# Planning the first sequence's start on one NeuronCore: two halves side by side, earlier constants

## The chip, the core and the metric

The kernel runs on one core of a Trainium2 chip. The core has five engines that run their own instruction streams in order and wait for one another by semaphores: TensorE (PE, matmuls), VectorE (DVE, elementwise work and scans), ScalarE (ACT, activations), GpSimd (POOL) and SyncE (SP), which here only starts DMA transfers. ScalarE and GpSimd start some transfers too. The metric is the device time of one execution in microseconds, and lower is better. The profiler's span runs from the first instruction to the last; a little lies around it.

## The reference

Eight sequences of 256 tokens with 512 features pass two layers. Each layer has a recurrence over time ("wkv") fed by a layer norm and a context, and a feed-forward block fed by another layer norm. In layer 0 the feed-forward block is a gated one whose down weights carry a Walsh-Hadamard transform; in layer 1 it is a mixture of 8 experts, of which each token uses two.

```python
x = x + tanh(g_xattn[0]) * wkv(w0, u0, layernorm(x), ctx)        # scan over 256 steps
x = x + tanh(g_ffn[0])   * ffn_hadamard(layernorm(x), W1, W2, W3) # hidden 2048
x = x + tanh(g_xattn[1]) * wkv(td1, tf1, layernorm(x), ctx)
x = x + tanh(g_ffn[1])   * experts(layernorm(x), gate_w, w1, w2, w3)  # top 2 of 8
```

One step of `wkv`, per channel:

```python
no = maximum(o, u + kt); A = exp(o - no); E = exp(u + kt - no)
y = (A * p + E * vt) / (A * q + E)
no2 = maximum(w + o, kt); A2 = exp(w + o - no2); E2 = exp(kt - no2)
p, q, o = A2 * p + E2 * vt, A2 * q + E2, no2
```

All is in float32. The Hadamard transform of 2048 values is folded into W2 on the chip, in two passes of 128x128 matrices: the first works on W2 in one layout of its rows and writes the result to a scratch tensor in DRAM, the second loads it back in the other layout.

## The kernel before

**Tiling.** Activations lie transposed: 512 features as 4 chunks of 128 partitions, tokens along the free side. Sequence 0 is worked in two blocks of 128 tokens (b = 0, 1; `NB` = 2), the later sequences whole. The recurrence of a block falls into two halves of two feature chunks each (hf = 0, 1); block 1 continues from the `carry` of block 0.

**Loads.** `load_first` (L218) brings x and the context of sequence 0, block by block, on SP's queue. Sixteen loads of W2 follow (L275), then the constants by `load_const` (L261), which are issued from ScalarE's queue, then W1 and W3 in sixteen pieces of 512 KB (`fill_w13`, L237, L241), then x of sequence 1 (`load_x`, L208). The stores of the first Hadamard pass into `turned` (L578), the loads from it (`fill_w2`, L249) and the clearing of the expert queues (`clear_queues`, L320) are on SP too.

**Steps.** `layernorm` (L374) is a chain through four engines: two adds on VectorE (L379, L381), a mean by a matmul (L385), a subtraction (L387), a Square on ScalarE (L391), two adds (L395, L397), a variance by a matmul (L404), an addition (L409), a power on GpSimd (L411), a transpose on TensorE (L416) and a product on VectorE (L418). `decayed_max` (L472) is one half of layer 0's recurrence: maximum scans (L490), a difference (L495), Relus and exponentials on ScalarE (L502 to L516), two clamps (L511), a product (L514), two scans (L519, L521) and a sum (L529); `attend` (L448) ends it with a reciprocal on VectorE (L460), two steps on GpSimd (L454, L456) and two more on VectorE (L464, L466). `transform` (L564) is one matmul of a Hadamard pass and its copy back by ScalarE (L570). `unit` (L739) is one hidden unit of the feed-forward block: eight matmuls (L746) and the gating on ScalarE and VectorE (L753, L755, L757).

**Order.** All these are generators that yield the engine and the estimated length of the next step. In a stretch under `tc.manual_schedule` the order in which the program writes the instructions is the order on the engines it names. For the first sequence's beginning (from L1303) that order is written out by hand: the norm of block 0, its halves step by step, then groups of first-pass Hadamard products between steps of the halves, with block 1's norm in between, then the norm of block 0 for the feed-forward block mixed with the beginnings of block 1's halves. `set_up` (L340) stands in the middle of it with the preparation of later constants. From L1330 on, a planner takes over. It keeps a `clock` for each engine and a list of `Line`s (L140), each one a generator with the time at which its next step can start. `product` (L192) writes the next matmuls of the feed-forward block and moves TensorE's clock on; `fill` (L176) then writes steps of the other engines that would start before that clock, the earliest first. `finish` (L184) writes a line to its end. The gating of a unit is a line put first in the list. For sequence 0 (`first_ffn_hidden`, L774) all sixteen units are computed for block 0, then `rest`, what is left of block 1's halves and its norm, is finished, and the sixteen units of block 1 follow, between which the second Hadamard pass is written. `ahead` is the recurrence and norm of the next sequence, `centre_gate` (L363) subtracts the mean of the expert gate's columns.

The hand-written order at its core:

```python
for n, hf in ((4, 0), (2, 0), (2, 1), (2, 0), (2, 1)):
    run(fw, n)            # n first-pass Hadamard products
    run(half[0][hf], 1)   # one stage of a half of block 0
    run(norm[1], 1)       # one stage of block 1's norm
```

Of the kernel before, what the change touches and what calls it, by code (L numbers as in the profile page):

```python
# [8 lines left out]
FP = mybir.dt.float32  # L9
# [41 lines left out]
def flamingo_kernel(  # L51
# [31 lines left out]
    def v4(name, shape=(P, DC, T)):  # L83
        return work.tile(list(shape), FP, tag="v4", name=name, bufs=35)
# [29 lines left out]

    clock = dict.fromkeys("PAVGD", 0.0)
    banks = [0.0, 0.0]
    lines = []
    LATER = 1e9  # L120
    SLACK = 0.8

    def pe(width, n=1, bank=False):
        return "P", n * max(0.28, 0.00169 * width), bank

    def dve(width, slope=1.0):
        return "V", 0.09 + 0.00105 * slope * width, False
# [9 lines left out]
    def dma(length):  # L137
        return "D", length, False

    class Line:  # L140
        def __init__(self, *gens, first=False):
            self.gen = chain(*gens)
            self.at = clock["P"]
            self.bank = None
            self.first = first
            lines.insert(sum(line.first for line in lines) if first else len(lines), self)
            self.go_on()


        def go_on(self):  # L150
            self.op = next((op for op in self.gen if op is not None), None)
            if self.op is None:
                lines.remove(self)

        def starts(self):
            return max(self.waits(), clock[self.op[0]])
# [4 lines left out]

        def write(self):
            engine, length, bank = self.op
            end = self.starts() + length
# [8 lines left out]
            self.go_on()  # L173


    def fill():  # L176
# [4 lines left out]
            lines[min(ready)[1]].write()  # L181


    def finish(line):  # L184
        while line in lines:
            if line.starts() >= LATER:
                next(other for other in lines if other.bank is not None).write()
            else:
                line.write()


    def product(length, write):  # L192
# [22 lines left out]
        return t  # L215


    def load_first():  # L218
        x[0], t = v4("x0"), v4("c0_0")
        for b in range(NB):  # L220
            bs = slice(b * P, (b + 1) * P)
            nc.sync.dma_start(out=x[0][:, :, bs], in_=x_in[:, :, bs])
            nc.sync.dma_start(out=t[:, :, bs], in_=ctx_in[:, :, bs])
        return t

# [32 lines left out]
    def w2_of(w, k):  # L258
        return w[k // 2][:, k % 2, :]
# [3 lines left out]
        nc.scalar.dma_start(out=t, in_=src)  # L263
        return t

    first_ctx = load_first()

    w2h = [new_w2(n) for n in "ab"]
    turned = dram.tile([H0, D], FP, name="turned")
# [3 lines left out]

    for i in range(16):
        nc.sync.dma_start(out=w2_of(w2h[i // KC], i % KC), in_=by_kj(W2T, i))  # L275
    wcol = [load_const(w0, [P, DC], "w0c"), load_const(td1, [P, DC], "w1c")]
    ucol = [load_const(u0, [P, DC], "u0c"), load_const(tf1, [P, DC], "u1c")]
    tgx = load_const(g_xattn.partition_broadcast(P), [P, 2], "tgx")
    tgf = load_const(g_ffn.partition_broadcast(P), [P, 2], "tgf")
    hadm = load_const(had, [P, P], "hadm")  # L280
    gate = load_const(gateT, [P, DC, NE], "gate")
# [52 lines left out]
    more_u = constant([P, DC], "more_u")  # L334

    nw0 = constant([P, DC], "nw0")
    nc.vector.tensor_scalar(nw0, wcol[0], -1.0, None, ALU.mult)


    def set_up():  # L340
        nc.vector.tensor_copy(token, token_i)


        nc.vector.tensor_tensor(had16, hadm, hadm[:, 112:113].to_broadcast([P, P]), ALU.mult)
# [6 lines left out]
        nc.scalar.activation(tgx, tgx, AF.Tanh)  # L351
        nc.scalar.activation(tgf, tgf, AF.Tanh)
        nc.vector.tensor_scalar(tgf_half, tgf[:, 1:2], 0.5, None, ALU.mult)

        nc.scalar.activation(wcol[1], wcol[1], AF.Exp)
        nc.vector.tensor_scalar(wcol[1], wcol[1], -1.0, None, ALU.mult)

        nc.scalar.activation(decay, wcol[1], AF.Exp)
        nc.vector.tensor_scalar(less, ucol[1], -1.0, 0.0, ALU.mult, ALU.min)
        nc.vector.tensor_scalar(more_u, ucol[1], 0.0, None, ALU.min)  # L360


    def centre_gate():  # L363
# [205 lines left out]
        yield act(D)  # L569
        nc.scalar.activation(w, ps, AF.Copy, scale=scale)  # L570

    def fwht_kj():
        for i in range(16):
            yield from transform(hadm, i, 1.0)
            if i % 4 == 3:
                lo = i - 3
                for m in range(lo, i + 1):
                    nc.sync.dma_start(out=by_kj(turned, m), in_=w2_of(w2h[m // KC], m % KC))  # L578
            yield

    latest_load = [None]

# [188 lines left out]

    def first_ffn_hidden(rest, fw):  # L774
        hs = [h1(T, f"t_f0_{k}") for k in range(2 * KC)]
        units = []
        for b in range(NB):
            bs = slice(b * P, (b + 1) * P)
            if b:
                fw = [Line(part) for part in fw]  # L780
            for k in range(0, 2 * KC, 2):
                for line in units[-6:-4] if len(units) >= 6 else []:
                    finish(line)
                ps = ps_gl.tile([P, 4, P], FP, tag="gl", name=f"gl_f0_{k}_{b}")
                gated = [
                    unit(
                        lambda c: xns[0][:, c, bs], *w13[j // KC], j % KC, P, f"f0_{j}_{b}", hs[j][:, bs],
                        ps[:, 2 * (j % 2) : 2 * (j % 2) + 2, :],
                    )
                    for j in (k, k + 1)  # L790
                ]
                units += [Line(g, first=True) for g in gated]
            if b < NB - 1:
                finish(rest)
        for part in fw:
            finish(part)
        return hs, units[-2 * KC :]
# [505 lines left out]
    fw = fwht_kj()  # L1303
    with tc.manual_schedule(engines={mybir.EngineType.PE, mybir.EngineType.Activation, mybir.EngineType.DVE}):
        take(norm[0])
        for hf in (0, 1, 0):
            run(half[0][hf], 1)
        set_up()
        run(half[0][1], 1)

        for n, hf in ((4, 0), (2, 0), (2, 1), (2, 0), (2, 1)):
            run(fw, n)
            run(half[0][hf], 1)
            run(norm[1], 1)
        take(fw)
        take(half[0][1])
        for hf in (0, 1, 0, 1, 0):
            run(norm_f[0], 1)
            run(half[1][hf], 1)

    def then_dispatch(s, before):
        finish(before)
# [192 lines left out]
```

## Time and profile before

| quantity | value |
|---|---|
| median of 3 runs | 1510.98 us (1508.51 to 1511.77) |
| the profiled execution's own time | 1514.42 us |
| its span | 1512.7 us, mean granted clock 0.986 |
| TensorE busy in the span | 1468.9 us (97%) |
| VectorE busy | 981.4 us (65%) |
| ScalarE busy | 288.3 us (19%) |
| first-pass Hadamard products (L568) | from 10.25 us to 33.1 us |
| first hidden product (L746) | 40.31 us |
| first hidden product of block 1 | 76.55 us |
| first down product of sequence 0 (L818) | 120.08 us |
| DMA rate, mean over 0 to 40.3 us | 335 GB/s |
| turned stores issued on SP | 34.1 to 50.8 us |
| turned loads issued on SP | 54.9 to 59.7 us |

A line of the timeline has the start, the length, the engine, the source line, the operation with what it writes and reads, and in brackets how long the engine stood idle before it and what ended that. A line of a table of stretches has the stretch, its length, the busy time of PE, weight loads (PEld), DVE, ACT and POOL with the number of instructions each, then the granted TensorE clock as a share of full speed, the busy share of the DMA engines, and GB/s.

### The profile page before, as it was taken

The numbers are of one execution on the slowest core, as the hardware profiler recorded it, in microseconds if no ns is written. First come the engines' busy times: TensorE is split into PE (matmuls) and PEld (weight loads), VectorE is DVE, ScalarE is ACT, GpSimd is POOL, SyncE is SP. The second block draws the span as 40 slices with busy tenths as digits, with TensorE's granted clock in tenths as the row PEclk, the third lists the DMA queues.
The fourth block names the chain that finished last, engine by engine and source line by source line (L and its number), as shares of the span: only waits on it lengthen the run. The fifth ranks groups of instructions, "written<-read, shape, count | busy, mean of one in ns | idle before, by whom it ended". The sixth has DMA issues, their size and how long they took to land. (4 is left out here: it accounts for less than half of the span.)

```text
span 1512.7 us, 19411 instructions
## 1 busy us (share of the span) xinstructions
PE 1468.9 (97%) x7336; PEld 1249.3 (83%) x7336; DVE 981.4 (65%) x2287; ACT 288.3 (19%) x676; POOL 240.2 (16%) x258
## 2 busy tenths in 40 slices
PE   5999999999999999999999999989999999999996
PEld 2979888888888888888877667778988889888894
DVE  6851786978789697876527423475747666476763
ACT  5240222213132221312111110011101111011110
POOL 1200121212122121312112210011301111010110
PEclk9899999999999999999999999999999999999998
DMA  9970011001100110115070313256114151240110
GB/s 332 357 248 15 1 36 50 29 28 43 42 29 28 50 35 15 43 27 183 15 250 29 100 36 120 68 191 213 60 62 176 40 203 43 93 150 28 59 32 18
DMA packets 79498, 135.16 MB, mean 89 GB/s; under 512 B 13084, under 2 KB 26524, under 8 KB 79392
## 3 DMA queue, kind: packets, MB, share of 16 engines
q1 hardware_dynamic: 69280, 108.45, 20.9%
q0 software_dynamic: 8960, 25.25, 4.8%
q8 instruction: 62, 1.02, 0.3%
q14 instruction: 44, 0.36, 0.1%
q10 hardware_dynamic: 1152, 0.09, 0.1%
HBM read 100.05 MB, written 37.90 MB: 91 GB/s over the span
## 5 line engine op out<-in xcount | busy, mean ns | idle before, releaser
L746 PE MATMUL gl_f<-xn,w_a 128*128 128x256 f32 (+1 forms) x1152 | 237.0, 361 | 1.6 <-DVE xn L418 1.6
L746 PEld LDWEIGHTS gl_f<-xn,w_a 128*128 128x128 f32 x1152 | 202.3, 194 | 27.7 <-issue 3.3
L746 PE MATMUL gl_f<-xn,w_b 128*128 128x256 f32 (+1 forms) x1152 | 223.9, 356 | 0.0
L746 PEld LDWEIGHTS gl_f<-xn,w_b 128*128 128x128 f32 x1152 | 199.0, 190 | 23.0
L729 PE MATMUL gl<-q,w_e 128*128 128x256 f32 x768 | 172.4, 382 | 6.6 <-DVEq L1425 3.8
L729 PEld LDWEIGHTS gl<-q,w_e 128*128 128x128 f32 x768 | 145.3, 192 | 27.2 <-issue 7.0
L917 POOL DMA_INDIRECT out<-g,who_e x40 | 43.7, 1092 | 506.8 <-DVE g L1179 412.8
L818 PE MATMUL o_f<-t_f,w_b 128*128 128x256 f32 x512 | 118.7, 380 | 0.0
L818 PE MATMUL o_f<-t_f,w_a 128*128 128x256 f32 x512 | 117.3, 380 | 0.0
L753 ACT ACTIVATE t_f<-gl_f 128x256 f32<-128x256 f32 (+1 forms) x144 | 49.8, 358 | 299.2 <-PE gl_f L746 298.6
L755 DVE SCALAR_TENSOR_TENSOR t_f<-t_f,gl_f 128x256 f32<-128x256 f32 (+1 forms) x144 | 53.8, 381 | 81.6 <-ACT t_f L753 81.4
L818 PEld LDWEIGHTS o_f<-t_f,w_b 128*128 128x128 f32 x512 | 96.2, 190 | 12.5
L818 PEld LDWEIGHTS o_f<-t_f,w_a 128*128 128x128 f32 x512 | 96.2, 190 | 12.5
L1104 PE MATMUL pa<-q,w_e 128*128 128x168 f32 x384 | 62.6, 306 | 0.0
L746 PE MATMUL gl<-q,w_e 128*128 128x256 f32 x256 | 61.1, 393 | 0.7 <-ACT q L868 0.7
L746 PEld LDWEIGHTS gl<-q,w_e 128*128 128x128 f32 x256 | 50.0, 198 | 12.0 <-issue 4.3
L1104 PEld LDWEIGHTS pa<-q,w_e 128*128 128x128 f32 x384 | 57.4, 190 | 1.8 <-issue 1.3
L1095 PE MATMUL y<-w_e,h 128*80 128x512 f32 (+1 forms) x128 | 56.9, 592 | 0.0
L909 POOL DMA_INDIRECT g<-out,who_e x40 | 45.1, 1126 | 61.5 <-DMA out<-g,who_e 23.2
L733 ACT ACTIVATE t<-gl 128x256 f32<-128x256 f32 x48 | 18.4, 383 | 190.4 <-PE gl L729 190.4
L757 DVE TENSOR_TENSOR t_f<-t_f,gl_f 128x256 f32<-128x256 f32 (+1 forms) x144 | 53.6, 381 | 0.7
L460 DVE RECIPROCAL e<-e 128x512 f32<-128x512 f32 (+1 forms) x18 | 53.9, 2992 | 0.1
(257 smaller groups left out, 2276.0 us busy)
## 6 DMA issues: line engine op xcount, KB each, us to landing
w_e<-in_w1T SPq DMA_DIRECT2D x32, 512.0 KB
w_e<-in_w3T SPq DMA_DIRECT2D x32, 512.0 KB
w_e<-in_w2T SPq DMA_DIRECT2D x32, 512.0 KB
queue<-empty SPq DMA_DIRECT2D x8, 1290.0 KB
r<-queue SPq DMA_DIRECT2D x32, 256.0 KB
c<-in_ctxT SPq DMA_DIRECT2D x15, 512.0 KB
out<-xr SPq DMA_DIRECT2D x16, 256.0 KB
x<-in_xT SPq DMA_DIRECT2D x7, 512.0 KB
```

The costliest lines, as they stand in the source:

```text
L460: nc.vector.reciprocal(den, den)
L729: nc.tensor.matmul(ps, lhsT=w13_of(w, c, k), rhs=xn(c)[:, :width], start=(c == 0), stop=(c == DC - 1))
L733: nc.scalar.activation(t, gp, AF.Tanh, scale=0.5)
L746: nc.tensor.matmul(ps, lhsT=w13_of(w, c, k), rhs=xn(c)[:, :width], start=(c == 0), stop=(c == DC - 1))
L753: nc.scalar.activation(t, gp, AF.Tanh, scale=0.5)
L755: nc.vector.scalar_tensor_tensor(t, t, 1.0, gp, ALU.add, ALU.mult)
L757: nc.vector.tensor_tensor(t, t, lp, ALU.mult)
L818: nc.tensor.matmul(o, lhsT=w2_of(w2h[k // KC], k % KC)[:, c * P : (c + 1) * P], rhs=hs[k], start=(k == 0), stop=(k == 2 * KC - 1),)
L909: nc.gpsimd.indirect_dma_start(out=g, out_offset=None, in_=out[:end, :], in_offset=bass.IndirectOffsetOnAxis(ap=who[:, b : b + 1], axis=0) ...
L917: nc.gpsimd.indirect_dma_start(out=out[:end, :], out_offset=bass.IndirectOffsetOnAxis(ap=who[:, b : b + 1], axis=0), in_=g, in_offset=None ...
L1095: nc.tensor.matmul(ys[b][:rows, :], lhsT=ts[k][:, b * P : b * P + rows], rhs=w2_of(w2, k), start=(k == 0), stop=(k == KC - 1),)
L1104: nc.tensor.matmul(ps[:, to, :], lhsT=weights[:, c, k * P : (k + 1) * P], rhs=toks[:, c, :], start=(c == 0), stop=(c == 1),)
```

## The change

The hand-written order of the beginning is replaced by the planner. A `Line` gets a level (0 is first), a start time of its own and functions to call when it ends. A new pseudo-engine "T" lets a line wait for a planned time (`until`). `joined(n, make)` makes a line when n others have ended. `alone` writes steps until the lines of the given levels are done: it looks for the step that could start first, and on that step's engine writes instead a step of a lower level number if that could start within 0.25 us. `near` and `least` are other estimates for this stretch alone (0.08 us between two steps of a line on one engine, 0.5 us at least for a matmul).

The lines are: the first norm of block 0, from 3.7 (level 0); both halves of block 0, from its end on, side by side (0); block 0's norm for the feed-forward block when both are done (0); the Tanh of g_xattn, from 7 (1); the first Hadamard pass in three lines, product i not before 12 + 0.8 i (1); block 1's first norm, from 22, its halves and its second norm (2); the rest of the set-up, from 45 (2). `alone(0, 1)` ends with levels 0 and 1; what is left of level 2 goes on behind the first products and is finished, by `finish_level(2)`, before block 1's. The order on GpSimd is fixed in this stretch too. The line of the next sequence starts at 46 or later, that of the gate's mean at 80. The program's order of loads becomes: block 0 of x and context; w0 and u0; a dummy activation; the Hadamard matrix and g_xattn; block 1; the other constants; then W2.

```diff
-    clock = dict.fromkeys("PAVGD", 0.0)
+    clock = dict.fromkeys("PAVGDT", 0.0)
+    near = [0.16]
+    least = [0.28]
+    WAIT = 0.25
     def pe(width, n=1, bank=False):
-        return "P", n * max(0.28, 0.00169 * width), bank
+        return "P", n * max(least[0], 0.00169 * width), bank
+    def until(time):
+        return "T", time, False
...
-        def __init__(self, *gens, first=False):
+        def __init__(self, *gens, first=False, level=3, at=None, then=()):
             self.gen = chain(*gens)
-            self.at = clock["P"]
+            self.at = clock["P"] if at is None else at
-            lines.insert(sum(line.first for line in lines) if first else len(lines), self)
+            self.level = 0 if first else level
+            self.then = then
+            lines.insert(sum(line.level <= self.level for line in lines), self)
...
+    def joined(n, make):
+        ends = []
+        def told(at):
+            ends.append(at)
+            if len(ends) == n:
+                make(max(ends))
+        return told
+    def finish_level(level):
+        while rest := [line for line in lines if line.level == level]:
+            finish(rest[0])
...
+    def alone(*levels):
+        while any(line.level in levels for line in lines):
+            start, i = min((line.starts(), i) for i, line in enumerate(lines))
+            next(
+                line for line in lines if line.op[0] == lines[i].op[0] and line.starts() <= start + WAIT
+            ).write()
...
-    first_ctx = load_first()
+    load_first(0)
+    w0c, u0c = load_const(w0, [P, DC], "w0c"), load_const(u0, [P, DC], "u0c")
+    early = const.tile([P, 1], FP, tag="early", name="early")
+    nc.vector.memset(early, 0.0)
+    nc.scalar.activation(early, early, AF.Square)
+    hadm = load_const(had, [P, P], "hadm")
+    tgx = load_const(g_xattn.partition_broadcast(P), [P, 2], "tgx")
+    load_first(1)
+    wcol = [w0c, load_const(td1, [P, DC], "w1c")]
+    ucol = [u0c, load_const(tf1, [P, DC], "u1c")]
+    tgf = load_const(g_ffn.partition_broadcast(P), [P, 2], "tgf")
+    gate = load_const(gateT, [P, DC, NE], "gate")
...
     for i in range(16):
         nc.sync.dma_start(out=w2_of(w2h[i // KC], i % KC), in_=by_kj(W2T, i))
-    wcol = [load_const(w0, [P, DC], "w0c"), load_const(td1, [P, DC], "w1c")]
...
-    def fwht_kj():
-        for i in range(16):
+    def fwht_kj(j):
+        for i in range(j, 16, 3):
+            yield until(12.0 + 0.8 * i)
             yield from transform(hadm, i, 1.0)
-            if i % 4 == 3:
-                lo = i - 3
-                for m in range(lo, i + 1):
-                    nc.sync.dma_start(out=by_kj(turned, m), in_=w2_of(w2h[m // KC], m % KC))
-            yield
+            nc.sync.dma_start(out=by_kj(turned, i), in_=w2_of(w2h[i // KC], i % KC))
...
-                finish(rest)
+                finish_level(2)
...
-    with tc.manual_schedule(engines={mybir.EngineType.PE, mybir.EngineType.Activation, mybir.EngineType.DVE}):
-        take(norm[0])
-        for hf in (0, 1, 0):
-            run(half[0][hf], 1)
-        set_up()
-        run(half[0][1], 1)
...
+    with tc.manual_schedule(engines=ordered):
+        near[0], least[0] = 0.08, 0.5
+        finals = [
+            joined(2, lambda at, b=b: Line(norm_f[b], level=2 * b, at=at)) for b in range(NB)
+        ]
+        second = [
+            joined(2, lambda at, hf=hf: Line(half[1][hf], level=2, at=at, then=(finals[1],))) for hf in range(2)
+        ]
+        def first_halves(at):
+            for hf in range(2):
+                Line(half[0][hf], level=0, at=at, then=(finals[0], second[hf]))
+        Line(norm[0], level=0, at=3.7, then=(first_halves,))
+        Line(norm[1], level=2, at=22.0, then=second)
+        Line(set_up_x(), level=1, at=7.0)
+        Line(set_up(), level=2, at=45.0)
+        turns = [Line(fwht_kj(j), level=1, at=0.0) for j in range(3)]
+        alone(0, 1)
+        near[0], least[0] = 0.16, 0.28
...
-            if s == 0:
-                rest = Line(half[1][1], half[1][0], norm_f[1])
             if s + 1 < NS:
-                ahead = Line(wkv(0, s + 1), ffn_norm(s + 1))
+                ahead = Line(wkv(0, s + 1), ffn_norm(s + 1), at=max(clock["P"], 46.0))
...
-            behind = Line(wkv(1, s - 1), then_dispatch(s - 1, behind), *rows) if s else Line(centre_gate())
-            hs, units = ffn_hidden(s) if s else first_ffn_hidden(rest, fw)
+            behind = Line(wkv(1, s - 1), then_dispatch(s - 1, behind), *rows) if s else Line(centre_gate(), at=80.0)
+            hs, units = ffn_hidden(s) if s else first_ffn_hidden(fw)
```

More of the change, by code (lines that the diff above doesn't have):

```diff
@@ L138, in dma @@
         return "D", length, False
+    def until(time):
+        return "T", time, False
     class Line:
-        def __init__(self, *gens, first=False):
+        def __init__(self, *gens, first=False, level=3, at=None, then=()):
             self.gen = chain(*gens)
-            self.at = clock["P"]
+            self.at = clock["P"] if at is None else at
             self.bank = None
-            self.first = first
-            lines.insert(sum(line.first for line in lines) if first else len(lines), self)
+            self.level = 0 if first else level
+            self.then = then
+            lines.insert(sum(line.level <= self.level for line in lines), self)
             self.go_on()
@@ L153, in go_on @@
                 lines.remove(self)
+                for told in self.then:
+                    told(self.at)
         def starts(self):
@@ L163, in write @@
             engine, length, bank = self.op
+            if engine == "T":
+                self.at = max(self.at, length)
+                self.go_on()
+                return
             end = self.starts() + length
@@ L173, in write @@
             self.go_on()
+            if self.op is not None and self.op[0] == engine:
+                self.at = end + near[0]
     def fill():
@@ L215, in load_ctx, with load_first @@
         return t
[L218 to L224, printed above, removed]
+    x[0], first_ctx = v4("x0"), v4("c0_0")
+    def load_first(b):
+        bs = slice(b * P, (b + 1) * P)
+        nc.sync.dma_start(out=x[0][:, :, bs], in_=x_in[:, :, bs])
+        nc.sync.dma_start(out=first_ctx[:, :, bs], in_=ctx_in[:, :, bs])
     def new_w13(name):
@@ L275, in flamingo_kernel @@
         nc.sync.dma_start(out=w2_of(w2h[i // KC], i % KC), in_=by_kj(W2T, i))
-    wcol = [load_const(w0, [P, DC], "w0c"), load_const(td1, [P, DC], "w1c")]
[L277 to L281, printed above, removed]
     w13 = [fill_w13(new_w13(n), *(w[:, i * HH : (i + 1) * HH] for w in (W1T, W3T))) for i, n in enumerate("ab")]
@@ L336, in flamingo_kernel, with set_up_x @@
     nw0 = constant([P, DC], "nw0")
-    nc.vector.tensor_scalar(nw0, wcol[0], -1.0, None, ALU.mult)
+    nc.vector.tensor_scalar(nw0, w0c, -1.0, None, ALU.mult)
+    def set_up_x():
+        yield act(2)
+        nc.scalar.activation(tgx, tgx, AF.Tanh)
     def set_up():
+        yield act(4)
+        nc.scalar.activation(wcol[1], wcol[1], AF.Exp)
+        yield act(2)
+        nc.scalar.activation(tgf, tgf, AF.Tanh)
+        yield dve(4)
+        nc.vector.tensor_scalar(wcol[1], wcol[1], -1.0, None, ALU.mult)
+        yield act(4)
+        nc.scalar.activation(decay, wcol[1], AF.Exp)
+        yield dve(4)
+        nc.vector.tensor_scalar(less, ucol[1], -1.0, 0.0, ALU.mult, ALU.min)
+        yield dve(4)
+        nc.vector.tensor_scalar(more_u, ucol[1], 0.0, None, ALU.min)
+        yield dve(1)
+        nc.vector.tensor_scalar(tgf_half, tgf[:, 1:2], 0.5, None, ALU.mult)
+        yield dve(16)
         nc.vector.tensor_copy(token, token_i)
+        yield dve(P)
         nc.vector.tensor_tensor(had16, hadm, hadm[:, 112:113].to_broadcast([P, P]), ALU.mult)
@@ L349, in set_up @@
             )
[L351 to L360, printed above, removed]
     def centre_gate():
@@ L770, in ffn_norm, with first_ffn_hidden @@
         yield from layernorm(x[s], xns[s], f"f_{s}")
-    def first_ffn_hidden(rest, fw):
+    def first_ffn_hidden(fw):
         hs = [h1(T, f"t_f0_{k}") for k in range(2 * KC)]
@@ L1302, in flamingo_kernel @@
     norm_f = [first_ffn_norm(b) for b in range(NB)]
-    fw = fwht_kj()
-    with tc.manual_schedule(engines={mybir.EngineType.PE, mybir.EngineType.Activation, mybir.EngineType.DVE}):
-        take(norm[0])
-        for hf in (0, 1, 0):
-            run(half[0][hf], 1)
-        set_up()
-        run(half[0][1], 1)
[L1311 to L1319, printed above, removed]
     def then_dispatch(s, before):
```

## The prediction

> **What bounds the kernel now.** I read the page's head and its slices first, then a table of stretches, then the timeline up to the first hidden products, then the clock in fine stretches. The page:
>
> ```profile
> span 1512.7 us, 19411 instructions
> ...
> PE 1468.9 (97%) x7336; PEld 1249.3 (83%) x7336; DVE 981.4 (65%) x2287; ACT 288.3 (19%) x676; POOL 240.2 (16%) x258
> ...
> PE   5999999999999999999999999989999999999996
> ```
>
> TensorE is busy everywhere but in the first slice and the last. So a microsecond is won where TensorE waits or runs slowly; elsewhere an earlier result waits in TensorE's own queue. The stretches (busy time by engine, granted clock at the end):
>
> ```profile
> 0.00:40.30 40.30, 22.10 (x47) 9.89 (x47) 26.39 (x95) 22.52 (x64) 6.80 (x19) 0.90 0.96 335
> 40.30:76.40 36.10, 35.90 (x276) 35.37 (x277) 30.34 (x73) 8.07 (x23) 7.25 (x8) 0.87 0.99 355
> 76.40:120.00 43.60, 43.60 (x299) 35.86 (x299) 23.17 (x57) 16.97 (x40) 3.16 (x3) 1.00 0.61 209
> 120.00:320.00 200.00, 200.00 (x964) 176.60 (x963) 138.57 (x276) 42.63 (x92) 31.46 (x29) 1.00 0.07 26
> ```
>
> From 40.3 us TensorE has no gap worth naming. Before it, a chain of small steps ends in the first block's normalised activations:
>
> ```profile
> 4.18 0.42 DVE L379 TENSOR_TENSOR s_k<-x 128x256 f32<-128x256 f32 x1 [0.71 <-DMA x<-in_xT]
> 5.71 1.28 ACT L391 ACT_TABLE_LOAD   x1 [5.71 <-DMA u0c<-in_u]
> 5.82 0.69 DVE L387 TENSOR_TENSOR k<-x,mean_k 128x512 f32<-128x512 f32 x1 [0.89 <-PE mean_k L385]
> 7.00 0.63 ACT L391 ACTIVATE sq_k<-k 128x512 f32<-128x512 f32 x1
> 10.50 0.69 DVE L418 TENSOR_TENSOR k<-k,rstd_k 128x512 f32<-128x512 f32 x1 [1.24 <-PE rstd_k L416]
> 23.77 0.69 DVE L519 TENSOR_TENSOR_SCAN q<-a,e 128x258 f32<-128x258 f32 x1
> 31.01 0.48 DVE L466 SCALAR_TENSOR_TENSOR x<-dd,tgx,x 128x256 f32<-128x256 f32 x1
> 39.58 0.68 DVE L418 TENSOR_TENSOR xn<-xn,rstd_f 128x512 f32<-128x512 f32 x1
> 40.31 2.08 PE L746 MATMUL gl_f<-xn,w_a 128*128 128x128 f32 x8 [1.59 <-DVE xn L418]
> ```
>
> Norm 0 ends at 11.2, block 0's recurrence at 31.5, its second norm at 40.3. The second half's scan at 23.77 had its inputs at 17.8 and stood behind block 1's norm in VectorE's order. The clock in stretches of 1 us:
>
> ```profile
> 35.00:36.00 1.00, 0.00 (x0) 0.00 (x0) 0.90 (x4) 1.00 (x4) 0.00 (x0) 0.91 1.05 387
> 36.00:37.00 1.00, 0.19 (x1) 0.22 (x2) 0.97 (x5) 0.97 (x4) 0.00 (x0) 0.50 1.03 381
> 48.00:49.00 1.00, 1.00 (x6) 1.00 (x6) 0.96 (x3) 0.00 (x0) 0.00 (x0) 0.50 1.07 406
> 49.00:50.00 1.00, 1.00 (x9) 1.00 (x8) 0.39 (x1) 0.12 (x1) 0.00 (x0) 0.77 1.03 387
> ```
>
> After the Hadamard products end at 33.1 the clock halves at 35.9 and returns at 49.5: the first 9 us of hidden products ran at half speed.
>
> **The change part by part.**
>
> *Table load and constants.* The dummy Square draws the 1.28 us table load between ScalarE's second and third constant transfer, at about 1.7 us. Square now waits for the table until 7.00 though k was ready at 5.82 + 0.69 = 6.51: -0.49 us. Six issues of at most 0.45 then run from about 3.2 to 5.9, ahead of 6.51; if two wait for earlier transfers, as SP's fourth issue waited for w0c by 0.9, Square is late by up to 1. The Tanh of g_xattn, planned at 7, waits for a transfer behind it in ScalarE's order, but nothing else is wanted there before 12. I take -0.5 (bounds -0.5 to +0.5).
>
> The Trainium skill speaks against this part: its page ScalarE: Activation LUTs, "What ACT_TABLE_LOAD costs", adds a 1.38 us drain to the 1.28 us load. Here Square starts at 7.00, right as the load ends at 6.99, so the row denies it; by the page the six issues would end at 7.3 and this part would cost 0.3 instead.
>
> *Halves side by side.* Per half VectorE does, start to start: memsets 0.1, two scans 0.77, difference 0.38, two clamps 0.56, product 0.38, two scans 1.19, sum 0.45, reciprocal 1.75, final two 0.93: 6.5 us. Two halves make 13.0; ScalarE's 2.3 and GpSimd's 1.4 us of one half lie under the other's. From norm 0's end at 10.7 this gives 23.7 against 31.5. Gone from between are block 1's norm (level 2), the set-up (0.8 us of ScalarE at 14.7 to 15.5, moved to 45) and the wait of 23.77.
>
> What comes in between: the plan starts one Hadamard product each 0.8 us from 12 at 0.865 us apiece; the trace's first ones take 1.75 (two instructions at 0.88: 10.25 to 15.5 for six), since TensorE is slow there. About four run so before it is fast; TensorE and the 0.6 us copies behind it on ScalarE then trail the plan by 2 to 3.5 us (four times 1.75 less 0.865), and what is queued behind those copies is the second half's exponentials, with 1 to 1.5 us of slack under the first half's reciprocal. I take +1.5 (0 to 5): ready at 25.2.
>
> *Second norm.* The first norm took 4.18 to 11.19, without the table 6.5; this one 8.7. Queued behind trailing Hadamard products on TensorE (two at 0.87) and an occasional lower-level VectorE step (0.4 to 0.7) I take 7.8 (6.5 to 8.7). First hidden product: 33.0 against 40.3, a gain of 7.3; with all ends good 30.2 (10.1), all bad 37.7 with a late Square (2.6).
>
> *Clock.* From 40.31 to 55.04 TensorE did 80 instructions of hidden products, the gate's mean and one norm's mean. At the full-speed 0.113 us (128 in 14.46) the 80 are 9.0; the gate's eight, at a weight load of 0.19 each, and the mean's two make some 1.6: 10.6 against 14.7, so half speed cost 4.1. With sixteen products from 12 on, the last ends near 29 (four slow, twelve at 0.86), and TensorE has only mean, variance and transpose until 33. In the old trace 33.1 to 36.8 empty was enough to halve it. A 4 us gap with 1 us of work is close to that row, so I keep 2.7 of the 4.1 (0 to 4.1).
>
> The Trainium skill's page TensorE: Matmul & The Clock Gate, Part 1, has it that a window of about 3.4 us with TensorE idle halves the clock and one busy window of that length restores it. Here 40.3 to 49.5 was busy throughout and took 9 us to be restored, so the row goes before the rule; by the rule a gap broken by three small products might keep the full clock, and the part would give 4.1.
>
> *Moves at nothing.* The gate's mean goes to plan time 80: eight instructions, 1.7 us, on TensorE in both. Set-up at 45: some 1.2 us of VectorE and 0.8 of ScalarE, needed by the second Hadamard pass (77.4 before) and by layer 1. The next sequence's norm is held until 46, because x1 landed at 43.6 (its VectorE step waited 1.5 for it). SP's queue: eight constants stand ahead of W2's sixteen issues in the order; each can hold W2's by about 1 us, as above, while W1/W3 for block 0 land long before 33. The sixteen turned stores are the same, now issued one by one instead of in fours, and stand behind the W1/W3 loads as before (34 to 51). Levels, `until` and `alone` cost no instruction.
>
> *What is late next.* Block 1's products start 29.0 (256 x 0.113) + 1.6 (small products) after block 0's: about 64.5, was 76.4; its norm ended at 64.4, 24 us after the first product. VectorE must do, from 33: half recurrences 13.0, norm 3.0, gating 8 x 0.96 = 7.7, set-up 1.2: 24.9 of 31. It fits: 0 (to 10).
>
> Sum: 7.3 + 2.7 = 10.0. Against the profiled execution's own 1514.42 (span 1512.7, 1.7 around it): 1504.4. That execution stood 3.4 above the median 1510.98, so the forecast is 1501.0. Its own range, from 10.1 + 4.1 to 2.6 + 0: 1496.8 to 1508.4.
>
> **Rivals.**
>
> *Block 1 starves (slower).* Held at level 3 but chosen by start time once products run, the next sequence's steps enter VectorE from 46: norm 4.7 and two recurrence halves of 11.3. If all 27.3 stand ahead of block 1's norm, it ends at 33 + 24.9 + 27.3 = 85, TensorE waits 20.7, less the gain: about 1521.7. It decides from a wait of 13 us. For: 5.9 us of slack only. Against: the old plan mixed the same work from 43.6 and ended at 64.4. 13%.
>
> *The trailing transforms eat it.* Every bad end of the chain holds and the clock falls again: 2.6 of gain, 1508.4. For: TensorE demonstrably slow from 10 to 22. Against: reciprocals hide 1 to 1.5 each. 13%.
>
> *The round trip of W2 becomes the bound.* Second-pass products are wanted from 65; the turned loads were issued at 54.9 to 59.7, and at 248, then 358 GB/s the first 2.1 MB land near 62, the rest near 68 (an estimate from those rates). A stream 5 us later, by constants holding SP, stalls TensorE 2 to 3: 1504. 6%.
>
> **How the numbers follow.** Forecast 68%. 0.2% (3.0 us) is about what a measurement of this kernel tells from no change: faster is below 1508.0. Faster: 66 + 6 + half of the second rival, 78%. Same: 9%. Slower: 11 from the first rival, 2 for later orders shifted by the plan's new clock: 13%. The range takes in the forecast's own, 1.8 below it for small terms set to nothing, and the second rival with 1.6 above: 1495 to 1510; what it leaves out is most of the first rival and the tails.
>
> **What would show it.** Table load near 1.7; block 0's last L466 at 24 to 27; first L746 at 31 to 35; clock 1.0 from there or halved for under 6 us; block 1's first product with no wait on L418; one stretch after it unchanged but shifted by 10. Wrong, if the first product stays past 38, or if its gain reappears as a TensorE wait between 60 and 80.

## The result, and the profile after

The changed kernel takes 1505.25 us (median of 12 runs, 1503.61 to 1509.52), the kernel before in the same comparison 1509.03 (1507.41 to 1513.58): a ratio of 0.9974 with a 95% interval of 0.9963 to 0.9986, some 4 us faster. The forecast was 10 us faster, 1501.0.

The profiled execution of the changed kernel took 1504.14 us. Its page, head and slices:

```profile
span 1502.4 us, 19409 instructions
...
PE 1460.9 (97%) x7336; PEld 1243.9 (83%) x7336; DVE 981.1 (65%) x2288; ACT 288.4 (19%) x677; POOL 245.2 (16%) x258
...
PE   6999999999999999999999999999999999999996
```

The span is 10.3 us shorter than in the profile before, more than the runs show. How much of it the change made is read from one stretch and the timeline. The stretch that took TensorE 35.90 us of work before, with the columns as before:

```profile
40.30:76.40 36.10, 33.18 (x257) 30.79 (x256) 29.23 (x84) 14.16 (x43) 6.02 (x8) 0.95 0.98 352
```

TensorE is now idle there for 2.9 us. The timeline has the beginning first, then that idle time (lines in between are left out):

```profile
1.73 1.28 ACT L309 ACT_TABLE_LOAD   x1 [1.73 <-PEq L1558]
7.56 0.49 ACTq L301 DMA_DIRECT2D gate<-in_gateT  x1
8.10 0.63 ACT L446 ACTIVATE sq_k<-k 128x512 f32<-128x512 f32 x1 [4.86 <-DMA w1c<-in_td]
25.33 0.48 DVE L521 SCALAR_TENSOR_TENSOR x<-dd,tgx,x 128x256 f32<-128x256 f32 x1
33.41 4.57 PE L798 MATMUL gl_f<-xn,w_a 128*128 128x128 f32 x24 [0.22 <-DVE xn L473]
...
45.52 0.69 DVE L434 TENSOR_TENSOR s_k<-x 128x512 f32<-128x512 f32 x1 [0.66 <-DMA x<-in_xT]
...
58.10 1.74 DVE L515 RECIPROCAL e<-e 128x256 f32<-128x256 f32 x1
59.76 0.35 DVE L452 TENSOR_TENSOR q_k<-q_k 128x256 f32<-128x256 f32 x1
60.26 0.58 PE L459 MATMUL var_k<-mean_m,q_k 128*128 128x1 f32 x4 [1.98 <-DVE q_k L452]
...
70.64 1.16 PE L798 MATMUL gl_f<-xn,w_a 128*128 128x128 f32 x8 [0.78 <-DVE xn L473]
...
115.19 3.62 PE L870 MATMUL o_f<-t_f,w_a 128*128 128x256 f32 x16
```

Block 0's recurrence ends at 25.8 (31.5 before), its second norm at 33.4 (40.3), and the first hidden product comes 6.9 us earlier. Square is later than before, at 8.10 instead of 7.00: it stands behind the transfer of the gate on ScalarE, which was issued at 7.56 only. At 60.26 the variance product of the *next* sequence's norm stands in TensorE's order among block 0's products. Its input comes from VectorE at 59.76, behind a reciprocal of block 1; TensorE waits 1.98 us. VectorE has worked without a pause since 45.52, where it took its first step on x of sequence 1 (x1) after waiting for that transfer. Block 1's first product waits another 0.78. Block 0's products take from 33.41 to 70.64, 37.2 us, where they took 36.2 before; block 1's, with the gate's mean now among them, 44.6 instead of 43.5. So the first down product stands at 115.19 instead of 120.08: 6.9 - 1.0 - 1.0 = 4.9 us.

The clock, in stretches of 1 us of the same execution:

```profile
34.00:35.00 1.00, 1.00 (x8) 1.00 (x7) 0.00 (x0) 0.00 (x0) 0.05 (x1) 0.57 1.04 383
37.00:38.00 1.00, 1.00 (x8) 1.00 (x8) 0.00 (x0) 0.00 (x0) 0.00 (x0) 0.72 1.06 389
61.00:62.00 1.00, 1.00 (x8) 0.78 (x6) 1.00 (x5) 0.00 (x0) 0.00 (x0) 0.73 0.89 309
64.00:65.00 1.00, 1.00 (x7) 1.00 (x6) 0.42 (x1) 0.39 (x1) 0.00 (x0) 0.57 1.03 395
```

It halves from 34.1 to 37.6, after the small products before the first hidden one, and again from 61.5 to 64.9, after the wait before 60.26. VectorE has nothing to do from 34 to 38: the transpose of block 1's norm, whose input was ready at 34.05, stands behind the first 24 hidden products in TensorE's order, at 37.82. What that costs was not tried. The remaining 5.4 us between the two spans arise past 770 us, where the profile before has two halved stretches of 6.8 us each (from 773.1 and 868.7) and this one has none there; the two profiles of one and the same kernel below differ in the same place, so that part isn't the change's.

### The profile page after: what moved, and what is told of

It is laid out like the page before. It is cut to its first block, busy times and chain, and to the rows that moved or that the text cites. A ratio compares the mean times of both kernels' runs of the same rounds, so it can differ in the third digit from the quotient of the medians.

```text
span 1502.4 us, 19409 instructions
## 1 busy us (share of the span) xinstructions
PE 1460.9 (97%) x7336; PEld 1243.9 (83%) x7336; DVE 981.1 (65%) x2288; ACT 288.4 (19%) x677; POOL 245.2 (16%) x258
```

## The experiments

Each is timed beside the kernel before, in one of three groups. The kernel before had a median of 1509.34 in the first group (the first four experiments below), 1510.88 in the group of "The planner's time not held" and "The changed kernel twice more", and 1509.42 in that of the other four. The ratios are to the kernel before of the same group; that of the changed kernel is 0.9974 (0.9963 to 0.9986).

**The next sequence held longer.** In the changed kernel:

```diff
-                ahead = Line(wkv(0, s + 1), ffn_norm(s + 1), at=max(clock["P"], 46.0))
+                ahead = Line(wkv(0, s + 1), ffn_norm(s + 1), at=max(clock["P"], 62.0))
```

> The changed kernel, with the next sequence's line held until plan time 62 instead of 46. Theory A (its norm's steps stand in TensorE's order among block 0's products and wait for VectorE): the wait of 2.0 us before var_k at 60.26 and the 0.8 us before block 1's first product go, the clock no longer halves at 61.7 (1.6 us); block 1's first product comes 36 to 34 us or less after block 0's instead of 37.2, and the first down product 3 to 4 us earlier than 115.2. Time some 1501.5 to 1502.5 against 1505.25. Rival B (VectorE is full anyway, the wait only moves): the same idle time before block 1's first product, and 1505 again.

Measured: 1502.5 us (1500.75 to 1507.2), 0.9947 (0.9930 to 0.9964) of the kernel before. The timeline at block 1's first product and at the first down product:

```profile
68.20 1.16 PE L798 MATMUL gl_f<-xn,w_a 128*128 128x128 f32 x8 [0.25 <-DVE xn L473]
...
112.70 3.62 PE L870 MATMUL o_f<-t_f,w_a 128*128 128x256 f32 x16
```

The wait of 1.98 is gone and that of 0.78 is 0.25; one of 0.73 for block 1's own norm has come in, at 59.92. The first hidden product was at 34.85 in this execution, so block 0's products took 33.4 us, and from the first hidden to the first down product it is 77.9 us instead of 81.8. That is 3.9 us, as theory A has it. Not all of it is the line's doing for sure: in another execution of the changed kernel itself (1503.41, below) the clock did not halve behind the wait, and there the same stretch takes 79.9 us, so that 2.0 us are left for the waits. The times agree with the gain: six of the eight lie below the fastest of the changed kernel's twelve.

**Four later constants on SP.** Their `load_const` moves behind the loop of W2's loads, with `nc.sync` instead of `nc.scalar`.

> The changed kernel, with the four later constants (td1, tf1, g_ffn, gate) issued on SP behind W2 instead of on ScalarE. Theory A (Square at 8.10 waits for ScalarE's issues, which wait for earlier transfers): Square starts at 6.5, the whole chain is 1.5 us earlier, the first hidden product at 31.9 to 32.3 instead of 33.4, time 1503.7 to 1504. Rival B (the chain is then held by the Hadamard products' pace from 12 on): Square at 6.5 but the first hidden product still past 33, time 1505.

Measured: 1505.86 us (1502.22 to 1509.81), 0.9967 (0.9951 to 0.9983). Square started at 6.50 and the first hidden product at 31.82, as theory A has it, but the time is that of rival B, though not for its reason:

```profile
6.50 0.63 ACT L446 ACTIVATE sq_k<-k 128x512 f32<-128x512 f32 x1 [3.27 <-DVE k L442]
...
31.82 4.57 PE L798 MATMUL gl_f<-xn,w_a 128*128 128x128 f32 x24 [0.22 <-DVE xn L473]
...
45.34 0.69 DVE L434 TENSOR_TENSOR s_k<-x 128x512 f32<-128x512 f32 x1 [2.08 <-DMA x<-in_xT]
...
60.09 0.58 PE L459 MATMUL var_k<-mean_m,q_k 128*128 128x1 f32 x4 [1.98 <-DVE q_k L452]
```

The products began 1.6 us earlier, and the wait for the next sequence's norm ends at 60.09 instead of 60.26. What sets that time is VectorE: its first step on x1 waits for the transfer (until 45.34 here, 45.52 in the changed kernel), and the variance product comes 14.74 us after that step. The distance is 14.74 or 14.75 us in all six profiles with the line at 46 (three of the changed kernel, and those of this, the next and the fourth experiment), and VectorE is busy in all of it up to its own step before the product. The step itself stands at 44.4 to 45.7; in three of the six it waits for the transfer. What is won in front of that step is waited away behind it.

**TensorE kept busy before the first product.** Two spare products, whose results nobody reads, stand behind the variance and the transpose of block 0's second norm:

```diff
+    def keep_busy(n):
+        for i in range(n):
+            ps = ps_o.tile([P, D], FP, tag="o", name="spare")
+            nc.tensor.matmul(ps, lhsT=hadm, rhs=empty[:, 0, :D], start=True, stop=True)
```

> The changed kernel, with two spare products of 512 columns on TensorE, one behind the variance and one behind the transpose of block 0's second norm. Theory A (the nearly empty gap of 30.5 to 33.4 halves the clock): the record shows full clock from 34 to 38, block 0's first 24 instructions take 2.8 instead of 4.4 us, time 1 to 1.7 below the changed kernel, 1503.5 to 1504.2. Rival B (the clock's windows run free, so that the gap halves it in some executions only): a smaller mean gain, 0 to 0.8, and a narrower spread of the times. If the spare products stand in the way, the first hidden product is up to 0.5 later.

Measured: 1504.3 us (1503.03 to 1506.17), 0.9956 (0.9940 to 0.9971). In the profile the first 24 instructions took 2.94 us instead of 4.57, at 35.18 us. That this is 1.8 us later than in the changed kernel's profile is not the spare products' doing: from the variance to the first hidden product it is 2.55 us in both. The Hadamard products before it ran later, with the clock halved from 19.8 to 23.2 here and not there. The times spread over 3.1 us, those of the changed kernel over 5.9. The gain of about 1 us by the medians is between A's and B's, and the intervals of the two ratios overlap. The narrower spread is what B forecast, but its reason isn't shown: the last experiment finds the spread of the changed kernel elsewhere.

**The old loads under the new plan.** The program order of loads and constants is put back and the dummy activation taken out.

> The changed kernel, with the loads and constants in the old program order and without the dummy activation; all the planning stays. Theory A (in the changed order ScalarE's issues held Square by 1.1 us, so this part costs): Square at 7.0, first hidden product at 32.3 to 32.8, time 1504 to 1504.7. Rival B (the Hadamard matrix and W2 arrive earlier in the new order and this carries part of the gain): the Hadamard products start or run later, first hidden product at 34 or later, time 1506 or more.

Measured: 1504.46 us (1502.19 to 1509.03), 0.9966 (0.9952 to 0.9980). Square stood at 7.08 and the first hidden product at 34.10:

```profile
34.10 2.94 PE L795 MATMUL gl_f<-xn,w_a 128*128 128x128 f32 x24 [0.21 <-DVE xn L470]
```

The time is A's, the first hidden product B's. That product doesn't decide: the clock was halved from 18.9 to 22.3 here, under the Hadamard products, as it was in one of three executions of the changed kernel itself. The part that moves the constants gains nothing that shows; the 0.8 us by which this kernel is faster in the medians is within its scatter. The line above shows a second thing: with no spare products and a gap as empty as the changed kernel's, the first 24 instructions ran at full speed, and the clock halved behind the wait at 59.63 instead (59.8 to 63.2).

**The kernel before, kept busy.** Six such spare products in the kernel before, four behind the mean and one behind each of the others.

> The kernel before, with six spare products of 512 columns on TensorE between the end of its Hadamard products and its first hidden product (four behind the mean, one behind the variance, one behind the transpose of block 0's second norm). Nothing else is changed. Theory A (the kernel before lost some 4 us to the halved clock after 33 us, in most executions): granted clock up from 0.9875 to about 0.990, first hidden product within 0.5 of 40.3, time 3 to 4.5 below the kernel before. Rival B (only the profiled execution had that, the usual one loses 1 or less): time within 1 of the kernel before.

Measured: 1513.39 us (1507.65 to 1516.98), 1.0022 (1.0011 to 1.0034): slower, which neither theory had. The timeline on TensorE:

```profile
40.23 1.16 PE L754 MATMUL gl_f<-xn,w_a 128*128 128x128 f32 x8 [0.95 <-DVE xn L426]
...
45.81 0.67 PE L390 MATMUL mean_k<-s_k,mean_m 128*128 128x256 f32 x2 [2.64 <-DVE s_k L386]
```

The same step in the kernel before, with VectorE's first step on x1:

```profile
43.56 0.69 DVE L379 TENSOR_TENSOR s_k<-x 128x512 f32<-128x512 f32 x1 [1.52 <-DMA x<-in_xT]
45.60 1.06 PE L385 MATMUL mean_k<-s_k,mean_m 128*128 128x256 f32 x2
```

The first hidden products run at full speed (1.16 us for eight instead of 2.08), and then TensorE waits 2.64 us for the next sequence's mean, whose x has only just landed; without a wait it stood at 45.60 in the kernel before. Behind that wait the clock halves after all, from 46.9 to 50.3:

```profile
47.00:48.00 1.00, 1.00 (x7) 1.00 (x6) 1.00 (x2) 0.00 (x0) 0.56 (x1) 0.50 1.05 404
```

The first down product is at 119.87 instead of 120.08. So the part of the halved clock that lies before x1's landing, some 2.4 of the 4.1 us that I had priced (2.9 us to the mean's place instead of 5.3), cost the kernel before almost nothing: what it slowed had to wait for x1 in any case. The part behind it came back in another place, so this run doesn't show what it is worth. Where this kernel loses 4 us by the medians was not settled. In the profiles it is 2.8 us slower past the first down product, all of it past 770; it has a wait of 3.0 us for the queue's rows at 773, where the profile before has 1.5.

**The planner's time not held.** The changed kernel with `at=clock["P"]` for the next sequence's line.

> The changed kernel with the next sequence's line free from the planner's own TensorE time on, as in the kernel before, instead of from 46. Theory (x of sequence 1 lands at 44 to 45 whatever stands before, and in the kernel before this, not the halved clock alone, set the first 5 us of hidden products): TensorE comes to the next sequence's mean after the first eight products, at 35 to 36, and waits for x1 until 45.5 to 46; the first down product stands at 119 to 121 as in the kernel before, time 1508 to 1511. Rival (the wait is short, because the planner writes the mean later or x1 comes earlier): first down product at 116 or earlier, time 1504 to 1506.

Measured: 1514.99 us (1513.13 to 1516.31), 1.0034 (1.0022 to 1.0046): slower than the kernel before, and worse than the theory had it.

```profile
43.79 0.69 DVE L434 TENSOR_TENSOR s_k<-x 128x512 f32<-128x512 f32 x1 [8.99 <-DMA x<-in_xT]
44.99 1.22 PE L440 MATMUL mean_k<-s_k,mean_m 128*128 128x256 f32 x2 [5.53 <-DVE s_k L436]
```

VectorE stands 9.0 us for x1, with block 1's halves and the gating queued behind it, and TensorE 5.5. All of the earlier start is lost at x1's landing, and block 1's norm then ends late too (its last step at 77.92), so that the first down product stands at 124.87, past the theory's 119 to 121. Holding that line until 46 is thus worth some 9 us, by the two ratios as by the medians; it is what lets the earlier first product count at all.

**The hand order alone.** In the kernel before, with its own loads, block 1's norm goes behind block 0's halves, the set-up behind that, and the next sequence's line is held for 14 us of plan time. The beginnings of block 1's halves, which the hand order had mixed with block 0's second norm, leave it as well and are left to the planner. Since the Tanh of g_xattn is part of the set-up, block 0's first recurrence is scaled by g_xattn[0] itself in this kernel.

```diff
-        set_up()
...
-            run(norm[1], 1)
...
-        for hf in (0, 1, 0, 1, 0):
+        for _ in range(5):
             run(norm_f[0], 1)
-            run(half[1][hf], 1)
+            run(norm[1], 1)
+        take(norm_f[0])
+        take(norm[1])
+        set_up()
...
+                ahead.at = max(ahead.at, 14.0)
```

> The kernel before, its loads and its hand-written order kept, but with block 1's first norm and the set-up moved behind block 0's halves, and the next sequence's line held for 14 us of plan time. Theory (most of the earlier first product comes from what stood between the two halves, not from the planner or the loads): first hidden product at 33 to 35, time 3 to 6 below the kernel before. Rival (the planner's interleaving of Hadamard copies and exponentials is what counts): first product at 37 or later, time within 2 of the kernel before.

Measured: 1503.96 us (1500.87 to 1511.34), 0.9960 (0.9944 to 0.9975), the first hidden product at 35.52. The time is the theory's. The first product is half a microsecond behind the theory's range and well ahead of the rival's 37: the moves alone bring 4.8 of the changed kernel's 6.9 us. The hold is in effect longer than the changed kernel's, too: the next sequence's mean stands at 54.19 instead of 46.86, and no wait for its variance is left. So moves and a hold, written by hand, reach the time of the planner's kernel; what each brings was not tried apart.

**Two and three edits together.**

> The changed kernel with the next sequence's line from 62 and the four later constants on SP. Theory (the earlier Square was absorbed alone because TensorE then waited at the same clock time, 60.1, for the next sequence's norm): with that wait gone the 1.6 us of an earlier first product carry to the first down product: it stands at 111 to 111.5 where the later line alone has 112.7, time 1501 to 1501.5. Rival (something else takes it): first down product at 112.5 or later, 1502.5.

Measured: 1502.78 us (1499.26 to 1508.27), 0.9959 (0.9944 to 0.9973); the first hidden product at 34.83, the first down product at 111.07. The first down product is where the theory has it, but not for its reason: the start at 6.45 did not carry to the first hidden product here, which followed slow Hadamard products (clock halved from 16.3 to 23.2). Instead the first 24 instructions ran at full clock (2.94 us), and with the wait at 60 gone the whole of that carried: block 0's products took 31.7 us instead of the 33.4 with the later line alone. No edit here keeps that clock up, so this is luck of the profiled execution. The median shows no gain over the later line alone.

> The changed kernel with all three edits: the next sequence's line from 62, the four later constants on SP, the two spare products. Theory (the wait behind the next sequence's norm, the halved clock and the late Square each stand on TensorE's path): the gains add up to 2.9 + 1 to 1.5 + 1, time about 1500 to 1501, spread below 2. Rival (the earlier Square is absorbed by a later wait, as it was alone): 1502.

Measured: 1500.35 us (1499.06 to 1500.57, six runs), 0.9937 (0.9920 to 0.9954).

```profile
33.49 2.94 PE L806 MATMUL gl_f<-xn,w_a 128*128 128x128 f32 x24
...
65.23 1.16 PE L806 MATMUL gl_f<-xn,w_a 128*128 128x128 f32 x8 [0.25 <-DVE xn L481]
...
109.73 3.62 PE L878 MATMUL o_f<-t_f,w_a 128*128 128x256 f32 x16
```

With the later line, the constants on SP and the spare products, block 0's products take 31.7 us and the first down product stands at 109.73, 5.5 us earlier than in the changed kernel. All of that is the shorter block 0 (37.2 us there): the first hidden product is no earlier, at 33.49, behind Hadamard products with the clock halved from 18.2 to 21.6. The time and the spread are the theory's, but that the earlier Square adds its 1 us isn't shown. This is the fastest of all kernels here, 9 us below the kernel before, with the narrowest times, though of six runs only.

**The changed kernel twice more,** to see where its two groups of times (eight from 1503.6 to 1506.6, four from 1508.7 to 1509.5) part.

> The changed kernel itself, for one more profiled execution. Theory (its times fall into two groups, about 1504 and 1509, by the clock in the gap before the first hidden products): an execution near 1509 shows the clock halved from about 31 to 34 on for two windows or more and the first down product 3 to 5 us later than 115.2; one near 1504 shows at most one halved window there. Rival: a halved clock elsewhere makes the group of 1509, with the first down product at 115 as before.

> The changed kernel itself once more, for the same question as the run before it: an execution near 1509 shows the clock halved for two windows or more between 31 and 45, one near 1504 at most one; the rival has the halved windows elsewhere.

Measured: 1509.81 and 1503.41, one of each group. Two stretches of each, 1509.81 first:

```profile
770.00:775.00 5.00, 4.67 (x11) 3.77 (x12) 0.00 (x0) 0.28 (x1) 0.00 (x0) 0.50 0.99 339
865.00:870.00 5.00, 4.94 (x21) 4.08 (x21) 3.67 (x11) 3.13 (x9) 2.88 (x5) 0.50 0.14 52
```

```profile
770.00:775.00 5.00, 5.00 (x23) 4.32 (x22) 1.89 (x3) 1.10 (x2) 0.00 (x0) 0.94 1.05 399
865.00:870.00 5.00, 5.00 (x20) 3.33 (x19) 1.01 (x2) 0.45 (x1) 3.09 (x3) 1.00 0.36 108
```

The first down products were at 115.53 and 112.88, 2.65 apart, and the spans 6.5. Of the 2.65, 1.3 are there at the first hidden product (34.29 and 33.03; the slower one had the clock halved from 17.6 to 21.0, the faster one not), the rest comes by the halved clock behind the wait at 60, which the faster one doesn't have. Both halved the clock in the same way after the first hidden product (24 instructions in 4.57). The larger part, 3.8 us, arises past 760, where the slower one halves its clock from 768.6 to 775.4 and from 864.1 to 871.0, and the faster only from 767.2 to 770.6: the rival's case. They follow short waits, at the same places as in the profile before; why one execution halves there and another doesn't was not tried.

## Why the prediction was wrong in size

- *What is late next: the step that failed.* "It fits: 0" added up VectorE's work from 33 on and found some 6 us to spare for block 1's norm. It counted them over the whole stretch, and it left out that the next sequence's norm has steps of its own in TensorE's order, where TensorE waits at the first one that is late, however much time block 1 has. The runs showed in its place: VectorE is idle from 34 to 38, takes up x1 when it lands at 45.52, and has no pause from there to the step before the variance product; TensorE waits 1.98 us for it and 0.78 us for block 1's norm, and in two of three profiled executions loses 1.2 to 1.4 us more to the halved clock behind the wait (10.4 and 10.6 us from the variance product to block 1's first product, 9.2 where the clock stays full). With the line from 62 on the wait of 1.98 is gone, the 0.78 is 0.25 and the time is 2.75 us lower. The prediction's own sign of being wrong, a wait of TensorE between 60 and 80, is what came. The first rival named the cause, the next sequence's steps competing from 46 on, but at another place and with 20.7 us.
- *Clock: counted on a path that it wasn't on.* I counted 2.7 of 4.1 us as gain. The change of the clock itself was near that: the changed kernel halves it once after the gap (1.63 us: 4.57 against 2.94, at each of its three profiles). But time won in front of x1's landing is waited away behind it, in the changed kernel as the run with the constants on SP shows, and in the kernel before: with the first hidden products at full speed TensorE waited 2.64 us for x1, and the first down product moved by 0.2. I had the row that says so, VectorE's wait for x1 at 43.56, and used it only for the changed kernel. Only with the line from 62 on do these 1.6 us reach block 1 (31.7 against 33.4 us for block 0).
- *Halves side by side, second norm: right, in part by luck.* Predicted 25.2 and 33.0 for the end of block 0's recurrence and the first hidden product, measured 25.8 and 33.4 (33.0 and 34.3 in the two more profiles). Underneath, the first norm ended 1.6 us later than forecast (12.3, not 10.7), the recurrence took 13.5 us instead of 14.5 and the second norm 7.5 instead of 7.8. The hand-ordered kernel shows that moving block 1's norm and the set-up out of the way makes most of the gain.
- *Table load and constants: wrong sign.* Predicted -0.5 with bounds of -0.5 to +0.5, measured +1.1 on Square (8.10 against 7.00; +0.5 and +0.7 in the two more profiles). The load itself went where I said, at 1.73; the transfers behind it on ScalarE waited for earlier ones longer than the 0.9 that I had seen on SP. In the trace the issue at 7.19 waits on the semaphore that block 1's x had used, and that at 7.56 on the Hadamard matrix's. With the constants on SP Square stood at 6.50, the forecast's value.
- *Gate's mean at nothing:* it moved from a place where TensorE would have waited for x1 at full speed anyway (the 2.64 us above) to one where it doesn't wait: 0.96 us at 77.75, a small loss. The 1.7 us that I gave for both kernels is its length at half clock.
- *The rest shifted unchanged: right.* From the first down product to the end it took 1387.2 us, and 1392.6 before; in the changed kernel's execution of 1509.81 it took 1392.6 as well. TensorE's steps up to 765 us keep the same distance from the first down product in all of these, so the difference arises behind, where the clock was halved twice before and not in the changed kernel's profile.
- *The sum:* block 1's first product came 5.9 us earlier instead of 10, the first down product 6.9 - 1.0 - 1.0 = 4.9 (4.6 and 7.2 in the two more profiles), and the time 4 us by the medians. Three smaller sums in the prediction don't come out either: 33.0 + 29.0 + 1.6 is 63.6 and not 64.5, 31 less 24.9 leaves 6.1 and not 5.9, and the worst end by its own bounds is 38.4 for the first hidden product, not 37.7. None of them changes the account.

## What to carry to other kernels

When an engine runs slowly before a wait, price the slowness only after asking what it would have waited for at full speed. An earlier start is worth what the next fixed arrival leaves of it: here a transfer's landing at 44 to 45.5, with 14.7 us of VectorE's work behind it, took back what lay in front of it, until the steps that wait for it were written later. That an engine's work fits into a stretch says nothing of when a step in the middle is done: ask from which moment on it has no pause. A small product of other work in an in-order queue is a wait for that work's whole chain; place it by when its input is sure, not by when it may start.

## What the runs showed of the hardware

The clock halved after gaps that were not empty: in the changed kernel TensorE was busy 0.22, 0.51 and 0.78 us of the three stretches of 1 us from 31 to 34, and the clock fell at 34.1, during dense products. A like gap doesn't always do it: with the old loads the three stretches had 0.52, 0.21 and 0.50 us, and the clock stayed full. Of the eight profiles of the changed kernel and its variants without spare products six halved there and two (the old loads; the later line with the constants on SP) did not; of the two with spare products none did. So that the spare products keep the clock up is likely, and not shown.

Two executions of one kernel also differ under the Hadamard products: halved from 17.6 to 21.0 in one and not in the other, with the first hidden product 1.3 us apart. Their times, 1509.81 and 1503.41, differ mainly by halved stretches (two of 6.8 us against one of 3.4) hundreds of microseconds behind the change, so a single profile's span is no measure of a change of 5 us.
